# A state-space layer with pairwise scan products, reciprocal roots by power, one ring of nine buffers, and transfer prices and tie-breaks in its planner

## The chip, the cores and the metric

The kernel runs on one core of a Trainium2 chip. The metric is device time in microseconds (us) of one execution; lower is better. Five engines run side by side, each through its own instruction stream in order: TensorE (PE; its weight loads are shown as PEld), VectorE (DVE), ScalarE (ACT), GpSimd (POOL) and SyncE (SP), which here issues nearly all transfers.

## The reference, cut to what matters

Eight images of 384 channels and 1024 positions go through a state-space block and a small MLP, then through a second MLP with sign-binarised weights. All is float32.

```
t = layernorm(layernorm_c(x))                       # (8, 1024, 384)
xm, z = split(t @ in_proj_w.T)                      # 768 each
xc = silu(causal_conv3(xm) + conv_b)
dt, Bm, Cm = split(xc @ x_proj_w.T, [24, 40])
dt = softplus(dt @ dt_proj_w.T + dt_proj_b)
h_t = exp(dt_t * A) * h_{t-1} + (dt * xc)_t * Bm_t  # 768 channels x 16 states
y = (sum_n h * Cm + xc * D) * silu(z)
x = x + gelu(y @ out_proj_w.T @ mlp_w1.T + b1) @ mlp_w2.T + b2
t = t + bitlinear(gelu(bitlinear(layernorm(t))))    # W = sign(W - mean of its group)
```

`bitlinear` scales its result by the largest magnitude within an image and clips it. There are five such groups of one image each, so the last step is done for images 0 to 4 alone.

## The kernel before

The kernel first lists all work as operations (`Plan.add`: engine, price in us, what it reads and writes, which buffers it takes), and `Plan.run` then simulates the engines and writes the instructions out in the order that it finds. Nothing reorders them on the chip. An operation has a lane and an image number; `rank` orders the ready ones by lane, image and place in the list. PE's sums of scan results come first (lane -1), then the scans (lane 0), fronts of the next images, the MLPs, and the binarised MLP. Prices come from `c_act`, `c_dve`, `c_pool` and constants; a transfer holds a common line for size / 395e3 and lands 0.9 us later. A `Ring` is a set of equal buffers; a `Piece` is a tile that takes one when its first operation is issued. Where PE would stand for over 0.7 us, filler matmuls (tile `spare`, L412) are put in to hold its clock.

The stages, for each image b and halves of 512 positions:

- `s1`, the front. `norm` (L543 on) sums over channels on PE, and gets the reciprocal root by ACT's Sqrt (L587) and DVE's reciprocal (L590) on a 128x128 tile. Then come in_proj, the convolution, and Silu in place on one tile of six channel blocks (128x3072); x_proj (`p_dbc`); `p_bc` (L703), which lays out B and C rows; dt_proj, six matmuls of 128 rows (L722), of which only 2 x 24 rows matter, and Softplus. POOL multiplies xc by dt in place, 512 columns at a time (L732). xc, z, dt and dtx go to DRAM in one transfer each.
- `s2`, the scan. A unit is two tiles; a tile holds 32 channels x 4 states on 128 partitions and 1024 positions (images 0 and 7 run in halves, two channel groups of 512 to a tile). dt and dtx are read back with each row repeated for four states, B and C rows with each repeated for 32 channels. Per unit and quad of states, for each tile: ACT's exponential into PSUM (`da`, two buffers, L510), POOL's product u = dtx * B (L886), DVE's scan (L890), and the product with C: on POOL where `on_pool` says so (L904, scan written to u), otherwise on DVE (L907, scan written to da). PE sums four states with 32-column matmuls (`py`, L842).
- `s3`, out_proj and the first MLP; `ffn`, the binarised MLP, which stores y1 in DRAM, waits for its maximum, loads it again (`gf`), clips on POOL and applies Gelu; `binarise`, once, early.

Images 0 to 7 pass through these overlapped: under the scan of one image lie the front of later ones and the MLPs of earlier ones.

Of the kernel before, what the change touches and what calls it, by code (L numbers as in the profile page):

```python
# [33 lines left out]
P = 128  # L34
# [8 lines left out]
HK = KH // 2  # L43
T = 512
# [41 lines left out]

def c_act(n):
    return 0.25 + n * 0.00084


def c_dve(n):
    return 0.19 + n * 0.00102

# [36 lines left out]
class Piece:  # L130
# [8 lines left out]

    def __getitem__(self, part):  # L140
        return self, part

# [13 lines left out]
class Op:  # L156
    __slots__ = (
        "engine", "cost", "emit", "prio", "slack", "table", "size",
        "wants", "next", "ready", "tiles", "others", "settle",
# [3 lines left out]
class Plan:  # L163
# [12 lines left out]
    def add(self, engine, cost, emit, r=(), w=(), claim=(), table=None, size=0, others=None):  # L176
# [3 lines left out]
        op.size, op.prio = size, (*self.prio, len(self.ops))  # L180
# [40 lines left out]
    def run(self):  # L221
# [22 lines left out]
        def choose(e, now, able):  # L244
            able = [op for s, op in able if s <= now]
            if e == "ACT":
                same = [op for op in able if op.table == table and table != "exp"]
                plain = [op for op in able if op.table in (None, "exp")]
                able = same if table is not None and same else plain or able
            if e in ("DVE", "POOL"):  # L250

                able = [op for op in able if op.prio[0] > 0 and op.ready <= now - PATIENCE] or [
                    op for op in able if op.prio[0] == 0] or able
            return min(able, key=rank)

        def rank(op):
# [11 lines left out]
            return (*first, op.prio[2])  # L268
# [13 lines left out]
        while left:  # L282
# [49 lines left out]
            if e == "SP":  # L332
                dma_free = max(dma_free, end + 1.0) + op.size / 395e3
                end = dma_free + 0.9
# [17 lines left out]
class Layer:  # L352
    def __init__(self, ctx, tc, a, out):
# [9 lines left out]
        def ring(tag, bufs, where=sbuf):  # L363
# [7 lines left out]
            "front": ring("front", 2), "t_f": ring("t_f", 2), "w_f": ring("w_f", 3),  # L371
            "dbc": ring("dbc", 1), "halo": ring("halo", 2),

            "dt_r": ring("dt_r", 3), "dtx_r": ring("dtx_r", 3), "u": ring("u", 9),
# [4 lines left out]
            "yg": ring("yg", 1), "hid": ring("hid", 2), "t_b": ring("t_b", 1), "w_b": ring("w_b", 3),  # L379
            "w6": ring("w6", 2), "w6_n": ring("w6_n", 2), "res": ring("res", 2),  # L380

            "t_n": ring("t_n", 2), "small": ring("small", 7),

            "mm": ring("mm", 3, psum), "sq": ring("sq", 1),
            "rstd": ring("rstd", 2),
# [6 lines left out]
        for b in range(B):  # L392
            for name in ("dt", "dtx"):
                self.dram[name, b] = handed(f"{name}_d{b}", [DI, L])
# [24 lines left out]

    def constants(self):
        nc, a, const = self.nc, self.a, self.const
        small = const.tile([P, 3], F32, name="small")
        one, self.eps_m, self.eps_f = (small[:, i : i + 1] for i in range(3))
        for at, value in ((one, 1.0), (self.eps_m, E1 * E2), (self.eps_f, E_FFN)):
            nc.vector.memset(at, value)
# [8 lines left out]
        self.pick = const.tile([P, 2 * NS], F32, name="pick")  # L436
        nc.vector.tensor_add(self.pick, ident[:, DQ : 2 * DQ], ident[:, DP + DQ : DP + 2 * DQ])
        self.edge = const.tile([P, KD, 2], F32, name="edge")
# [23 lines left out]
    def load(self, to, view, src, r=(), size=0, cost=0.4):  # L462
# [3 lines left out]
            size=size,  # L466
        )

    def store(self, dst, frm, view, w, size, cost=0.4):
# [6 lines left out]
    def rows_moved(self, t, parts, move, r, w):  # L476
        n = P // len(parts)
        for i, mem in enumerate(parts):
            self.plan.add(
                "SP", 0.35, lambda i=i, mem=mem: move(t.real[i * n : (i + 1) * n, :], mem),  # L480
# [3 lines left out]
    def weights(self, ring, k, src, r=()):  # L484
        w = self.piece(ring, [P, k, P], ring)
        self.load(w, lambda t: t, src, r=r, size=4 * P * k * P, cost=0.34)
        return w

    def matmuls(self, p, w, t, k0, n, start, stop, r, claim, w0=0):


        def emit():
            for k in range(n):
                self.nc.tensor.matmul(  # L494
                    p.real, w.real[:, w0 + k, :], t.real[:, k0 + k, :],
# [47 lines left out]
    def norm(self, t, eps, scale):  # L543
# [17 lines left out]
        def spread(src, name):  # L561
            p = self.piece("mm", [P, T], name)

            def emit():
                for g in range(G):
                    one = self.ident[:, g * DQ : g * DQ + 1].to_broadcast([P, P])
                    nc.tensor.matmul(
                        p.real[:, g * TG : (g + 1) * TG], one, src.real, start=True, stop=True
# [16 lines left out]
        rstd = self.piece("rstd", [P, TG], "rstd")  # L585
        self.act(
            lambda: rstd.real, lambda: p_var.real, AF.Sqrt, c_act(TG), r=[p_var], w=[rstd],  # L587
            table="sqrt", bias=eps, scale=scale,
        )
        add("DVE", 0.93, lambda: nc.vector.reciprocal(rstd.real, rstd.real), w=[rstd])  # L590
        p_r = spread(rstd, "p_r")
# [6 lines left out]
    def s1(self, b):  # L598
# [3 lines left out]
        r_t, r_w, r_z, r_x = ("t_n", "w_b", "yg", "hid") if b == 1 else (  # L602
            "t_f", "w_f", "front", "front")

        def by_pair(name, half, t):
            d = self.dram[name, b]
            self.store(d.real[:, half].rearrange("k p l -> p k l"), t, lambda x: x, [d[half]],
                       4 * P * KD * T)

        def tiled(name, half, t):  # L610
            d = self.dram[name, b]
            to = d.real[:, HALVES[half]].rearrange("(k p) l -> p k l", p=P)
            self.store(to, t, lambda x: x, [d[half]], 4 * P * KD * T)

        def normed(half):
            t = self.piece(r_t, [P, KC, T], "t")
            src = a["x"][b][:, HALVES[half]].rearrange("(k p) l -> p k l", p=P)
            with self.plan.lane(14 if b == 1 else 4):
                self.load(t, lambda x: x, src, size=4 * P * KC * T)
                self.norm(t, self.eps_m, (1.0 + E2) / C)  # L620
# [7 lines left out]
        def gate(half, t):  # L628
            z = self.piece(r_z, [P, KD, T], "z")
            for m in range(KD):  # L630
                w = self.weights(r_w, KC, a["in_proj_w"][KD + m])
                pm = self.mm3(w, t, [t[k] for k in range(KC)], [z], "p_z")
                self.affine(
                    lambda m=m, z=z: z.real[:, m, :], lambda pm=pm: pm.real, [pm], [z[m]]
                )
            all_z = [z[m] for m in range(KD)]
            self.act(lambda z=z: z.real, lambda z=z: z.real, AF.Silu, c_act(KD * T),
                     r=[], w=all_z, table="silu")
            by_pair("z", half, z[0])

        for half, cols in enumerate(HALVES):
# [3 lines left out]
            xc = self.piece(r_x, [P, KD, T], "xc")  # L645
            for m in range(KD):
                w = self.weights(r_w, KC, a["in_proj_w"][m])
                pm = self.mm3(w, t, [t[k] for k in range(KC)], [xc], "p_in")
                tap = [self.conv_w[:, m, j : j + 1] for j in range(3)]
                self.affine(  # L650
                    lambda m=m, xc=xc: xc.real[:, m, :], lambda pm=pm: pm.real, [pm], [xc[m]],
# [7 lines left out]
                for s in (1, 2):  # L659
                    add("DVE", c_dve(T) + 0.06, lambda m=m, xc=xc, pm=pm, s=s, tap=tap: (  # L660
                        nc.vector.scalar_tensor_tensor(  # L661
                            xc.real[:, m, s:], pm.real[:, : T - s], tap[2 - s],
                            xc.real[:, m, s:], ALU.mult, ALU.add,
                        )
                    ), r=[pm], w=[xc[m]])
            if half:
                def edge(xc=xc):
                    tmp = self.edge
                    for s in (1, 2):
                        tp = tmp[:, :, :s]  # L670
                        w = self.conv_w[:, :, 2 - s : 3 - s].to_broadcast([P, KD, s])
                        nc.gpsimd.tensor_mul(tp, halo.real[:, :, 2 - s :], w)
                        nc.gpsimd.tensor_add(xc.real[:, :, :s], xc.real[:, :, :s], tp)

                add("POOL", 1.5, edge, r=[halo[m] for m in range(KD)],
                    w=[xc[m] for m in range(KD)])
            all_m = [xc[m] for m in range(KD)]
            self.act(lambda xc=xc: xc.real, lambda xc=xc: xc.real, AF.Silu, c_act(KD * T),
                     r=[], w=all_m, table="silu")
            by_pair("xc", half, xc[0])  # L680


# [4 lines left out]
            def low(w=w, xc=xc, p_dbc=p_dbc):  # L687
                for k in range(KC):
                    for i in range(2):
                        nc.tensor.matmul(  # L690
                            p_dbc.real[i * DP : (i + 1) * DP, :],
                            w.real[:, k, i * DP : (i + 1) * DP], xc.real[:, i * KC + k, :],
# [5 lines left out]
            p_bc = self.piece("mm", [P, TG], "p_bc")  # L698
            rows = self.piece("rstd", [P, TG], "rows")

            def both_halves(dbc=dbc, p_bc=p_bc):
                for g in range(G):
                    nc.tensor.matmul(  # L703
                        p_bc.real[g * DQ : (g + 1) * DQ, :], self.pick,
                        dbc.real[:, g * TG : (g + 1) * TG], start=True, stop=True,
                    )

            add("PE", 0.45, both_halves, r=[dbc], w=[p_bc], claim=[rows])
            self.affine(
                lambda rows=rows: rows.real, lambda p_bc=p_bc: p_bc.real, [p_bc], [rows], n=TG  # L710
            )
            d = self.dram["rows", b]
            for g in range(G):
                at = slice(cols.start + g * TG, cols.start + (g + 1) * TG)
                self.store(d.real[:, at], rows, lambda x, g=g: x[g * DQ : (g + 1) * DQ, :],
                           [d[half, g]], 4 * DQ * TG)
            dt = self.piece(r_x, [P, KD, T], "dt")
            for k in range(KD):
                if k % KC == 0:
                    w = self.weights(r_w, KC, a["dt_proj_w"][k // KC])  # L720
                pd = self.piece("mm", [P, T], "p_dt")
                add("PE", MM, lambda k=k, pd=pd, dbc=dbc, w=w: nc.tensor.matmul(  # L722
                    pd.real, w.real[:, k % KC, :], dbc.real, start=True, stop=True,
                ), r=[dbc, w], w=[pd], claim=[dt])
                self.affine(
                    lambda k=k, dt=dt: dt.real[:, k, :], lambda pd=pd: pd.real, [pd], [dt[k]],
                    self.dt_b[:, k : k + 1],
                )
            self.act(lambda dt=dt: dt.real, lambda dt=dt: dt.real, AF.Softplus, c_act(KD * T),
                     r=[], w=[dt[k] for k in range(KD)], table="softplus")  # L730
            for k in range(KD):
                add("POOL", c_pool(T), lambda k=k, xc=xc, dt=dt: nc.gpsimd.tensor_mul(  # L732
# [539 lines left out]
```

## Time and profile before

| | us |
|---|---|
| median of 3 runs | 3261.21 (3260.56 to 3263.69) |
| the profiled execution's own time | 3262.23 |
| its span, first to last instruction | 3260.4 |
| mean granted clock of PE | 0.984 |
| HBM traffic | 566 MB read, 180 MB written, 229 GB/s |
| ACT: 222 table loads | 284.8 |
| DVE: scans of 1024 / of 512 | 1310.2 / 470.4 |
| PE: products of p_h, p_o, p_out, p_in, p_z and both p_y | 2454.2 |
| PE: py, and fillers | 376.6, 80.0 |

Busy time is a sum over the instructions of a row; the engines work at the same time, so rows of different engines don't add. The lines of the profile themselves are shown with the steps that use them.

### The profile page before, as it was taken

How to read it: one execution, taken by the hardware profiler on the slowest of the kernel's cores; microseconds unless marked ns; L12 is line 12 of the kernel's file. 1: busy time of each engine (PE TensorE's matmuls, PEld its weight loads, DVE VectorE, ACT ScalarE, POOL GpSimd, SP SyncE). 2: the span in 40 equal slices, each digit the busy share in tenths (PEclk: the TensorE clock that was granted, in tenths of full speed). 3: DMA queues.
4: the chain of work that ended last, by engine and by line, in shares of the span. 5: the costliest groups of instructions: out<-in, count | busy, mean ns of one | idle time of the engine just before them, and what ended most of it. 6: DMA issues, size and time to landing. Idle time of an engine off the chain costs nothing.

```text
span 3260.4 us, 34027 instructions
## 1 busy us (share of the span) xinstructions
PE 3122.5 (96%) x11098; PEld 1317.7 (40%) x11098; DVE 2742.3 (84%) x2127; ACT 2024.3 (62%) x2246; POOL 2848.7 (87%) x1371
## 2 busy tenths in 40 slices
PE   8988999999999999999899999999999999999999
PEld 4333433444433434334334344343443534433334
DVE  4778899799978899888998878999788988789880
ACT  4778787656665576665656566755666565656551
POOL 1688899979999989999989999989999899999970
PEclk9998999999999999999999999999999999999999
DMA  6988778657796568675686667866677656766542
GB/s 218 305 282 276 249 250 294 221 183 234 259 322 197 184 230 291 229 238 197 208 298 211 237 211 246 295 225 226 220 275 250 207 185 205 249 187 207 167 141 76
DMA packets 367345, 748.73 MB, mean 230 GB/s; under 512 B 33856, under 2 KB 111168, under 8 KB 367168
## 3 DMA queue, kind: packets, MB, share of 16 engines
q1 hardware_dynamic: 366736, 746.46, 68.5%
q8 instruction: 89, 1.46, 0.2%
q14 instruction: 88, 0.72, 0.1%
q10 hardware_dynamic: 432, 0.09, 0.0%
HBM read 566.06 MB, written 180.36 MB: 229 GB/s over the span
## 4 chain that ended last, share of the span: by engine, by line
PE 74%; DMA 9%; DVE 6%; ACT 5%; issue 2%; POOL 2%; SPq 1%; ACTq 0%; DVEq 0%; POOLq 0%
PE p_y L494 17%; PE p_o L494 14%; PE p_h L494 13%; PE py L842 9%; PE p_out L494 6%; PE p_z L494 6%; PE p_in L494 5%; DVE da L890 2%; DMA w<-in_out_proj_w 2%; DMA w_f<-in_in_proj_w 2%; DVE u L890 1%; ACT L510 1%; DMA w_b<-in_mlp_w 1%; ACT da L510 1%; PE spare L412 1%
## 5 line engine op out<-in xcount | busy, mean ns | idle before, releaser
L886 POOL TENSOR_TENSOR u<-dtx_r,bc 128x1024 f32<-128x1024 f32 x768 | 1790.4, 2362 | 72.3 <-DMA dtx_r<-dtx_d 46.3
L510 ACT ACTIVATE da<-dt_r,a_neg 128x1024 f32<-128x1024 f32 (+1 forms) x960 | 902.7, 945 | 534.0 <-DVE u L907 331.1
L904 POOL TENSOR_TENSOR u<-u,bc 128x1024 f32<-128x1024 f32 x352 | 828.4, 2364 | 121.5 <-DVE u L890 115.5
L890 DVE TENSOR_TENSOR_SCAN da<-da,u 128x1024 f32<-128x1024 f32 (+1 forms) x416 | 840.5, 2020 | 111.6 <-POOL u L886 62.9
L890 DVE TENSOR_TENSOR_SCAN u<-da,u 128x1024 f32<-128x1024 f32 (+1 forms) x352 | 699.5, 2010 | 90.3 <-ACT da L510 63.0
L494 PE MATMUL p_h<-t,w_b 128*128 128x512 f32 x1152 | 513.6, 600 | 10.9 <-DMA w_b<-in_mlp_w 9.9
L907 DVE TENSOR_TENSOR u<-da,bc 128x1024 f32<-128x1024 f32 x416 | 507.9, 1221 | 10.5 <-ACT state L901 0.3
L494 PE MATMUL p_o<-g,w 128*128 128x512 f32 x1152 | 506.7, 595 | 5.4 <-ACT g L510 2.9
L842 PE MATMUL py<-u,fold 128*32 128x512 f32 x3072 | 376.6, 605 | 4.5 <-DVE u L907 4.5
L494 PEld LDWEIGHTS p_h<-t,w_b 128*128 128x128 f32 x1152 | 214.7, 190 | 298.1 <-issue 256.4
L494 PEld LDWEIGHTS p_o<-g,w 128*128 128x128 f32 x1152 | 215.9, 190 | 292.0 <-issue 277.3
L494 PE MATMUL p_y<-tn,w_b 128*128 128x512 f32 x720 | 324.9, 598 | 4.0 <-DVE tn L592 3.3
L494 PE MATMUL p_y<-gf,w_n 128*128 128x512 f32 x720 | 319.0, 599 | 6.7 <-DMA w_n<-bin_w 4.0
L510 ACT ACT_TABLE_LOAD x222 | 284.8, 1283 | 11.7 <-DVE xc L661 7.3
L494 PE MATMUL p_out<-yg,w 128*128 128x512 f32 x552 | 249.2, 604 | 8.9 <-DMA w<-in_out_proj_w 4.3
L494 PE MATMUL p_z<-t,w_f 128*128 128x512 f32 x504 | 232.5, 611 | 8.2 <-DMA w_f<-in_in_proj_w 6.2
L494 PE MATMUL p_in<-t,w_f 128*128 128x512 f32 x504 | 228.3, 602 | 10.8 <-DMA w_f<-in_in_proj_w 8.6
L494 PEld LDWEIGHTS p_y<-gf,w_n 128*128 128x128 f32 x720 | 135.1, 191 | 187.6 <-issue 172.4
L494 PEld LDWEIGHTS p_y<-tn,w_b 128*128 128x128 f32 x720 | 133.9, 190 | 183.9 <-issue 155.4
L842 PEld LDWEIGHTS py<-u,fold 128*32 128x32 f32 x3072 | 81.5, 110 | 261.1 <-issue 203.2
L525 ACT ACTIVATE g<-p_h,v_vecs 128x512 f32<-128x512 f32 x157 | 106.3, 681 | 120.9 <-PE p_h L494 120.7
L525 ACT ACTIVATE y<-p_y,v_vecs 128x512 f32<-128x512 f32 x138 | 94.1, 683 | 130.0 <-PE p_y L494 100.3
(112 smaller groups left out, 2700.3 us busy)
## 6 DMA issues: line engine op xcount, KB each, us to landing
dtx_r<-dtx_d SPq DMA_DIRECT2D x144, 512.0 KB, 5.8
dt_r<-dt_d SPq DMA_DIRECT2D x144, 512.0 KB, 6.0
w_b<-in_mlp_w SPq DMA_DIRECT2D x192, 192.0 KB, 2.9
w<-in_mlp_w SPq DMA_DIRECT2D x96, 384.0 KB, 3.6
w_f<-in_in_proj_w SPq DMA_DIRECT2D x168, 192.0 KB, 4.2
y_d<-y SPq DMA_DIRECT2D x120, 256.0 KB, 3.4
gf<-y_d SPq DMA_DIRECT2D x20, 1536.0 KB, 9.5
xc_d<-xc SPq DMA_DIRECT2D x16, 1536.0 KB, 7.3
```

Of the source, the lines that this page charges most:

```text
L412: self.plan.fill = lambda: self.nc.tensor.matmul(self.plan.spare.real[:, : 2 * P], self.ones, self.one.to_broadcast([P, 2 * P]), start=Tru ...
L494: self.nc.tensor.matmul(p.real, w.real[:, w0 + k, :], t.real[:, k0 + k, :], start=start and k == 0, stop=stop and k == n - 1,)
L510: lambda: self.nc.scalar.activation(out(), in_(), func, **{k: v() if callable(v) else v for k, v in kw.items()}),
L525: nc.scalar.activation(out(), in_(), AF.Identity, bias=bias, scale=scale)
L842: nc.tensor.matmul(py.real[p0 : p0 + DQ, :], self.fold, hc, start=False, stop=(q == NQUAD - 1), skip_group_check=True,)
L886: add("POOL", 2.36, lambda: nc.gpsimd.tensor_mul(u.real, dtx_r.real, spread(bq)), r=[dtx_r, bq], w=[u])
L890: add("DVE", (0.2 if half else 0.15) + n * 0.00209, lambda k=k, col=col: nc.vector.tensor_tensor_scan(to.real[:, k, :], da.real[:, k, :], ...
L904: add("POOL", 2.36, lambda: nc.gpsimd.tensor_mul(u.real, u.real, spread(cq)), r=[cq], w=[u])
L907: add("DVE", 1.21, lambda: nc.vector.tensor_mul(u.real, da.real, spread(cq)), r=[da, cq], w=[u])
```

## The change

Tiles of a unit become *pairs*: the two tiles' values lie interleaved, `[P, wide, n, 2]`, so that one POOL instruction multiplies both by one row of B or C, each element of which is used twice. dtx is stored interleaved too (`[KC, P, 2 * L]`) and read back in one transfer; a unit's channels are now every fourth one of 256. The scan reads and writes every other element. The fourth quad's u is written over dtx. `on_pool` gives POOL quads 0 and 2, and quad 1 in every fourth unit.

In `norm` the variance is scaled, turned by a small matmul to 128x4, an epsilon added, and raised to -0.5 on POOL; its spread uses the 128x4 columns as weights. dt_proj uses 32 rows per matmul, two at a time on different rows. The tiles of six blocks become three pieces of two (`Split`), with activations in place, stores and loads by piece; hid, yg and image 1's z share one ring of nine such pieces. `p_bc` and its four stores become one matmul (`p_all`) and one store. The column sums in `binarise` are taken three or four at a time. `gf` waits for its own y1 only. The planner gets transfer prices by kind (`land`), and `TURNS`: a number for each stretch of 100 us of planned time shifts an operation's place in the list by up to 16.

```diff
+STRETCH, REACH = 100, 16
+TURNS = (
+    19522, 59978, 49910, 0, 34827, 0, 6565, 14275, 0, 7565, 33371, 19911,
...
+def turned(n, by):
+    x = ((n + 1) * 2654435761 + by * 40503 * 65537) & 0xFFFFFFFF
+    x = ((x ^ x >> 15) * 2246822519) & 0xFFFFFFFF
+    return (x ^ x >> 13) % (2 * REACH + 1) - REACH
...
+def c_pair(n):
+    return 0.19 + n * 0.00188
...
-            return (*first, op.prio[2])
+            return (*first, op.prio[2] + (turned(op.prio[2], turn) if turn else 0))
...
-                dma_free = max(dma_free, end + 1.0) + op.size / 395e3
-                end = dma_free + 0.9
+                dma_free = max(dma_free, end + 0.5) + 0.05 + op.size / 360e3
+                end = dma_free + op.land
...
-            "front": ring("front", 2), "t_f": ring("t_f", 2), "w_f": ring("w_f", 3),
+            "front": ring("front", 7), "t_f": ring("t_f", 2), "w_f": ring("w_f", 3),
...
-            "dt_r": ring("dt_r", 3), "dtx_r": ring("dtx_r", 3), "u": ring("u", 9),
+            "dt_r": ring("dt_r", 3), "dtx_r": ring("dtx_r", 2), "u": ring("u", 3),
...
-            "yg": ring("yg", 1), "hid": ring("hid", 2), "t_b": ring("t_b", 1), "w_b": ring("w_b", 3),
-            "w6": ring("w6", 2), "w6_n": ring("w6_n", 2), "res": ring("res", 2),
+            "hid": ring("hid", 9), "t_b": ring("t_b", 1), "w_b": ring("w_b", 3),
+            "w6": ring("w6", 2), "w6_n": ring("w6_n", 2), "res": ring("res", 4),
...
+        rstd = self.piece("root", [P, G], "rstd")
+        add("DVE", 0.1, lambda: nc.vector.tensor_scalar_add(rstd.real, p_turned.real, eps),
+            r=[p_turned], w=[rstd])
+        add("POOL", 0.8, lambda: nc.gpsimd.tensor_tensor(
+            rstd.real, rstd.real, self.power.to_broadcast([P, G]), ALU.pow
+        ), w=[rstd])
...
+        def in_place(t, func, table):
+            parts = [t[k] for k in range(KD)]
+            for p, piece in enumerate(t.pieces):
+                mine = parts[p * PER : (p + 1) * PER]
+                self.act(lambda piece=piece: piece.real, lambda piece=piece: piece.real, func,
+                         c_act(PER * T), r=parts if p == 0 else mine, w=mine, table=table)
...
+                def two(k=k, pds=pds, dbc=dbc, ws=ws):
+                    for i in range(2):
+                        rows = slice(i * DQ, (i + 1) * DQ)
+                        nc.tensor.matmul(
+                            pds[i].real, ws[i].real[rows, (k + i) % KC, :], dbc.real[rows, :],
+                            start=True, stop=True,
+                        )
...
+                dtx = self.piece("sq", [P, T, 2], "dtx")
+                add("POOL", 2.35, lambda p=p, dtx=dtx, xc=xc, dt=dt: nc.gpsimd.tensor_mul(
+                    dtx.real.rearrange("p n i -> p i n"), xc.pieces[p].real, dt.pieces[p].real
...
-        return q == 0 or (q == 2 and (i == 0 or m % 3))
+        return q % 2 == 0 or (q == 1 and m % 4 == 0)
...
+        def product(t, x, row):
+            nc.gpsimd.tensor_mul(
+                u.real[:, x], t.real[:, x], row.real.unsqueeze(2).to_broadcast([P, n, 2])
+            )
```

## The prediction

> **What bounds the kernel now.** I read the engine totals first, then the chain of waits, then the busy time by stage, and last single groups and stretches of the timeline. Times are microseconds (us).
>
> ```profile
> PE 3122.5 (96%) x11098; PEld 1317.7 (40%) x11098; DVE 2742.3 (84%) x2127; ACT 2024.3 (62%) x2246; POOL 2848.7 (87%) x1371
> PE 74%; DMA 9%; DVE 6%; ACT 5%; issue 2%; POOL 2%; SPq 1%; ACTq 0%; DVEq 0%; POOLq 0%
> ```
>
> TensorE (PE) is nearly always busy and makes up three quarters of the chain that ends last. The stages (PE, PEld, DVE, ACT, POOL busy, then clock, DMA share, GB/s):
>
> ```profile
> 0.00:105.00 105.00, 90.77 (x444) 46.50 (x446) 43.04 (x61) 51.89 (x63) 12.67 (x18) 0.97 0.74 245
> 105.00:400.00 295.00, 265.03 (x1000) 111.27 (x998) 252.52 (x246) 229.11 (x309) 255.35 (x161) 0.95 0.83 272
> 400.00:1200.00 800.00, 769.47 (x2868) 322.36 (x2865) 714.99 (x536) 526.53 (x568) 734.95 (x339) 0.99 0.71 237
> 1200.00:2000.00 800.00, 768.54 (x2657) 317.76 (x2656) 701.50 (x498) 491.75 (x489) 753.41 (x343) 0.98 0.71 239
> 2000.00:2800.00 800.00, 779.63 (x2803) 337.36 (x2802) 698.09 (x493) 485.27 (x490) 742.29 (x339) 0.99 0.68 231
> 2800.00:3180.00 380.00, 372.61 (x1157) 148.71 (x1156) 329.17 (x294) 223.59 (x313) 350.09 (x175) 1.00 0.60 186
> 3180.00:3260.00 80.00, 76.50 (x180) 33.76 (x178) 3.00 (x4) 16.12 (x17) 0.00 (x0) 1.00 0.24 73
> ...
> 1200.00:1300.00 100.00, 94.21 (x356) 40.34 (x355) 96.68 (x76) 68.08 (x74) 95.77 (x45) 0.95 0.83 284
> ...
> 2000.00:2100.00 100.00, 91.36 (x420) 39.90 (x419) 95.96 (x69) 68.65 (x70) 88.23 (x46) 0.95 0.78 270
> 2100.00:2200.00 100.00, 98.62 (x343) 39.87 (x342) 94.89 (x76) 57.16 (x71) 89.61 (x39) 1.00 0.67 230
> ```
>
> Three parts follow. The head, 0 to 105, is the front of image 0 before the first scan product. The tail from 3180 is the last half image's MLP, which waits for the last scan. Between lie 3075 us in which the scans run on POOL, DVE and ACT under the matmuls. There PE is busy 265.0+769.5+768.5+779.6+372.6 = 2955 us, but the filler matmuls (tile spare, 80.0 us in all, 71.2 of it here) are gaps in disguise: real work is 2884, 93.8% of the stretch, and 191 us are gaps. POOL is busy 2836 (92.2%), DVE 2696 (87.7%). So PE sets the pace, with POOL close behind. PE's dips (91 and 94 us of 100) fall where DVE stands at 96 to 97 and the fronts load (270 to 284 GB/s).
>
> **The change, part by part.** The rows I price from:
>
> ```profile
> L886 POOL TENSOR_TENSOR u<-dtx_r,bc 128x1024 f32<-128x1024 f32 x768 | 1790.4, 2362 | 72.3 <-DMA dtx_r<-dtx_d 46.3 <-PE py L842 21.6 <-issue 2.4
> L904 POOL TENSOR_TENSOR u<-u,bc 128x1024 f32<-128x1024 f32 x352 | 828.4, 2364 | 121.5 <-DVE u L890 115.5 <-PE p_in L494 1.0 <-POOL u L886 0.6
> L1088 POOL TENSOR_SCALAR gf<-gf,q 128x3072 f32<-128x3072 f32 x20 | 57.9, 2898 | 11.2 <-DMA gf<-y_d 10.5 <-DVE u L890 0.7
> ...
> L907 DVE TENSOR_TENSOR u<-da,bc 128x1024 f32<-128x1024 f32 x416 | 507.9, 1221 | 10.5 <-ACT state L901 0.3
> L590 DVE RECIPROCAL rstd<-rstd 128x128 f32<-128x128 f32 x26 | 24.2, 937 | 1.8 <-ACT rstd L510 1.3
> ```
>
> Two stretches of PE's timeline and the last long piece of the chain (start, duration, group):
>
> ```profile
> 290.68 1.92 PE L842 MATMUL py<-u,fold 128*32 128x512 f32 x16
> 293.64 0.43 PE L703 MATMUL p_bc<-dbc,pick 128*32 128x128 f32 x8 [1.03 <-ACT dbc L523]
> ...
> 3194.70 30.90 PE p_h L494 x72
> ```
>
> The last of them gives the price of a full 128x512 product: 30.90/36 = 0.858 us (each is two instructions). The py line is eight 32-column products, four side by side: 1.92 against 2 x 0.858 = 1.72, so a group of narrow products costs 0.2 over its streaming time.
>
> *Pairs on POOL.* Before: 768 first and 352 second products, 2618.8 us. After: two channel groups interleaved in one tile. A full image has 48 pairs of first products and 24 + 3 of second ones (quads 0 and 2, and quad 1 of every fourth unit), 75 instructions of 2048 elements; six images make 450. Images 0 and 7 run in halves, 24 + 14 pairs a half, two instructions of 1024 a pair: 304 instructions. No row shows a product whose second operand repeats each element twice. From above by the plain rows: 1024 elements 2362, 512 elements 1275 (L732), so 2.123 ns an element and 0.188 fixed; 2048 take 4.54, and the sum is 450 x 4.54 + 304 x 2.362 = 2759, 140 more than before, because more second products go to POOL. From below by the one-operand row L1088, 0.943 ns an element: 2048 take 2.1. Between them stands the price that the planner is given in the diff, 0.19 + 0.00188 n, 4.04. Its other prices stand within 1% of their rows (1.21 for L907's 1.221, 0.93 for L590's 0.937, 2.36 for L886's 2.362), and a repeated operand should lie below the plain rate and above the one-operand rate, nearest the plain one. I take 4.04 (2.12 for 1024): 450 x 4.04 + 304 x 2.12 = 2461, so -158, with both ends kept for the range. The Trainium skill, page "GPSIMD Engine Reference", section "Elementwise — side-by-side cycle accounting", speaks against this: it puts a two-input product at about 2.6 cycles of 1.2 GHz an element whatever the operands, as both inputs share one read port; the 2.123 ns above are 2.55 cycles, so the trace agrees for plain operands, and by it a pair would cost about 4.6. What that makes of the time is the slow rival below.
>
> *Other POOL work.* The powers: 26 of 128x4; between a tiny POOL instruction (0.21, edge row) and a scan product (2.4); I take the planner's 0.8, +21. The dt product as 48 of 1024 instead of 96 of 512: 48 x 2.36 against 118.6, -5. Edges 48 instead of 32 at 0.21: +3. POOL in the stretch: 2836 - 158 + 19 = 2697.
>
> *DVE.* Products after the scan: 21 pairs a full image and 10 a half, two products each, give 6 x 42 + 4 x 20 = 332 instead of 416, 84 x 1.221 = -103. The 26 reciprocals (24 us) become 128x4 additions at some 0.15: -20. Scans are as many as before; they now step over every other element of u. If that cost 10% of a scan it would be +150 and DVE the bound; nothing in the rows suggests it, so I take 0. DVE in the stretch: 2573.
>
> *ACT.* A hundred in-place activations of 3072 (2.77) become 300 of 1024, about 1.05 by the 1536 row (1.48) and the 512 copies: +37. Gone are 26 roots (9) with 26 to 52 table loads of 1.28 (33 to 67). Near nothing, on an engine 62% busy; the cover is its 38% idle.
>
> *PE.* dt: 96 products (82.4) become 48 groups of two on different rows; if they run side by side, 48 x 1.06 = 50.9, -31 (bounds 0, if they queue, and -41). No row shows row groups side by side; the py line shows column groups so. p_bc 0.43 becomes one full product: 16 x 0.43 = +7. Sums of the binarised weights three or four at a time: 9 x 0.858 + 12 x 0.644 to 3 x 1.06 + 3 x 0.84, -10. The turn of the variance: 26 tiny products with a weight load (0.19) and drain, about 0.3, +8 (2 to 15). Together -26: real work 2858.
>
> *Norm chain.* Out go root, its load and reciprocal (2.6 us), in come a scale, a product, an addition and the power, which in POOL's order can sit behind one pair (4.0); behind it queue the next scan products, for which DVE waits. PE waited 10.5 us for rstd in 6 of 26 norms; 6 x 4 more would be +24 at worst. I take 0 over the gaps below, since the rest are made well ahead.
>
> *Rings, transfers, order.* The product of dt is no longer made in place but in the single buffer sq, so one must be stored (5.8, a 512 KB landing) before the next is made; this lies in fronts made ahead, except for image 0. There the scan now starts after one product and one 512 KB store instead of six products (7.7) and 1.5 MB (7.3): 7.7 - 2.4 + 7.3 - 5.8 = 7 us earlier, head 98. u holds 3 pairs and the last one lies in dtx: 4 pairs where 9 tiles held 4.5; POOL waited 21.6 us for PE to free u, and doubling that is +22 on an engine with 8% idle. SP issues 2092 transfers now and 164 more then (+128 for stores by pair, +120 for the halves' rows, +68 loads of yg and gf, +16 weights, -168 for rows, dt, dtx), at 0.33 to 0.53 each some +70 on a queue that mostly stands waiting for buffers; bytes grow 3 MB of 749. Hidden behind the weights' lead; without it DMA's 9% of the chain (290) grows by the same 8%, +23. The planner's new transfer prices and turned ties add no instruction. They can close or open gaps, at most those 191 us; I give them 0 by themselves.
>
> **Sum.** What remains is how the gaps answer. DVE loses 123 us (4.6%) and POOL 139 (4.9%), the two that are full where PE dips. In the undisturbed 100 us (2100) PE has 1.4 idle, so gaps are not PE's own. I take a third off: 191 to 125. Stretch 2858 + 125 = 2983; head 98, tail 80.4: span 3161. The profiled execution took 3262.2 for a span of 3260.4, 1.8 around it, and stands 1 us above the median of the runs. Forecast 3163. POOL would then be 90% busy in the stretch, DVE 86%, which leaves room.
>
> **Rivals.** *Gaps stay in proportion* (only PE's own work counts): 2858/0.938 = 3047, + 180 = 3227. For it: PE's gaps are scattered over dozens of small waits for weights, activations and norms, which the change does not shorten. Against: the dips where DVE is full.
>
> *Gaps almost close*, as in the best stretches (98.5% PE): 2858/0.985 = 2901, total 3083. For it: fillers between 2000 and 2800 alone are 46 us and show PE waiting for scans; against: the weights' transfers stay as they are.
>
> *POOL becomes the bound (slower).* The pair costs the plain rate, 4.54. POOL's stretch is 2836 + 140 + 22 = 2998. It has never been over 98.8% in 100 us and hardly over 95% over 800; at 96% the stretch is 3123 and the time 3305 (3270 at 97.2%, 3340 at 95%). It decides from the point where POOL's 2697 grow to 0.96 x 3075 = 2952, by 255 over 602 pairs, 0.42: a pair of 4.46. For it: the measured plain rate; against: the planner's price. By the Trainium skill's page cited above (about 4.6) this rival would hold.
>
> *The pairs on PE do not overlap and the ring of three pairs starves POOL:* +31 and +22 on the forecast, 3216, inside the range.
>
> **Chances.** Forecast 0.66 (own range 3105 to 3220), gaps in proportion 0.13, gaps close 0.08, POOL bound 0.11, and 0.02 for no change. A measurement of this kernel tells about 0.2% (6.5 us) from none. Faster 0.66 + 0.13 + 0.08 = 0.87, from which I give 0.01 to no change: 0.86, 0.03, 0.11. The range 3095 to 3250 leaves out the POOL rival and half of the one where gaps close.
>
> **What would show it.** Right: POOL products of 128x2048 near 4.04 and POOL below 2760 busy; 332 DVE products at 1.22 and scans still at 2.28; p_dt pairs of four instructions at 1.06; no reciprocal of 128x128; fillers and idle of PE together near 150 (218 now). Wrong: pairs over 4.46, POOL at 96% from 105 on and PE waiting on py; scans slower than 2.3; PE waiting for rstd over 30 us.

## The result, and the profile after

The changed kernel takes 3186.9 us (median of 4 runs, 3184.6 to 3200.4) against 3262.5 before: ratio 0.977, 95% interval 0.975 to 0.979. The forecast was 3163, range 3095 to 3250. So the sign and the range held, and 76 of the 99 us forecast came. The reason that I gave for most of them did not hold alone, as the experiments show.

Engine totals after, in the columns of the first fence of the prediction (the profiled execution took 3184.6, its span is 3182.5):

```profile
PE 3083.4 (97%) x10972; PEld 1274.9 (40%) x10972; DVE 2644.0 (83%) x2081; ACT 1966.5 (62%) x2363; POOL 2744.8 (86%) x1046
```

The groups that answer to the priced ones (line, engine, output and inputs, form, count; busy us and mean ns; idle before and what ended it):

```profile
L942 POOL TENSOR_TENSOR u<-dtx_r,bc 128x2048 f32<-128x2048 f32 x216 | 880.6, 4088 | 107.2 <-PE py L907 66.7 <-issue 22.5 <-DMA bc<-rows_d 8.1
L942 POOL TENSOR_TENSOR u<-u,bc 128x2048 f32<-128x2048 f32 x162 | 661.5, 4087 | 45.3 <-DVE u L967 45.3
...
L644 POOL TENSOR_TENSOR rstd<-rstd,small 128x4 f32<-128x4 f32 x26 | 26.4, 1016 | 31.1 <-DVE rstd L642 28.9 <-DVE mean L1146 1.4 <-DMA y_d<-y 0.9
...
L967 DVE TENSOR_TENSOR_SCAN u<-da,u 128x1024 f32<-128x1024 f32 x324 | 738.9, 2284 | 94.5 <-POOL u L942 48.7 <-ACT da L556 35.0 <-ACT z L556 0.8
L987 DVE TENSOR_TENSOR dtx_r<-da,bc 128x1024 f32<-128x1024 f32 x144 | 174.6, 1222 | 2.9
...
L451 PE MATMUL spare<-small 128*128 128x256 f32 x228 | 58.1, 394 | 0.0
L783 PE MATMUL p_dt<-dbc,w_f 32*128 32x512 f32 x168 | 55.1, 690 | 5.3 <-ACT dbc L569 2.7 <-DVE tn L628 1.1 <-DVE t L648 1.0
```

A pair costs 4.088, the scan still 2.284, the power 1.016, and POOL now waits for PE to free u (66.7 in this row alone, 21.6 in the corresponding row before). The stages in which the scans run in full (columns as in the prediction):

```profile
400.00:1200.00 800.00, 779.07 (x2879) 319.78 (x2877) 692.54 (x522) 514.38 (x600) 703.23 (x236) 0.98 0.73 246
1200.00:2000.00 800.00, 789.60 (x2814) 325.84 (x2812) 697.52 (x505) 480.79 (x525) 735.35 (x227) 1.00 0.73 245
2000.00:2800.00 800.00, 794.30 (x2708) 328.21 (x2707) 695.49 (x504) 497.69 (x554) 750.58 (x245) 1.00 0.73 245
```

PE stands at 97 to 99% there, 96 to 97% before. I split PE's time into real work (busy less fillers) and gaps (idle plus fillers). Before: 3122.5 - 80.0 = 3042.5 work, 3260.4 - 3042.5 = 218 gaps. After: 3025.3 and 157. So of 78 us of span, 17 are work and 61 are gaps; the question is what closed the gaps.

### The profile page after: what moved, and what is told of

Same layout as the page of the kernel before. It is cut to its first block, busy times and chain, and to the rows that moved or that the text cites. A ratio compares the mean times of both kernels' runs of the same rounds, so it can differ in the third digit from the quotient of the medians.

```text
span 3182.5 us, 33759 instructions
## 1 busy us (share of the span) xinstructions
PE 3083.4 (97%) x10972; PEld 1274.9 (40%) x10972; DVE 2644.0 (83%) x2081; ACT 1966.5 (62%) x2363; POOL 2744.8 (86%) x1046
## 5 line engine op out<-in xcount | busy, mean ns | idle before, releaser
L942 POOL TENSOR_TENSOR u<-dtx_r,bc 128x2048 f32<-128x2048 f32 (+1 forms) x360 | 1185.5, 3308 | 124.9 <-PE py L907 79.7
L942 POOL TENSOR_TENSOR u<-u,bc 128x2048 f32<-128x2048 f32 (+1 forms) x274 | 900.1, 3290 | 86.9 <-DVE u L967 81.4
L967 DVE TENSOR_TENSOR_SCAN u<-da,u 128x1024 f32<-128x1024 f32 (+1 forms) x436 | 869.1, 2007 | 127.1 <-POOL u L942 71.4
L967 DVE TENSOR_TENSOR_SCAN da<-da,dtx_r 128x1024 f32<-128x1024 f32 (+1 forms) x192 | 386.3, 2019 | 55.6 <-POOL dtx_r L942 34.2
L942 POOL TENSOR_TENSOR dtx_r<-dtx_r,bc 128x2048 f32<-128x2048 f32 (+1 forms) x120 | 396.8, 3311 | 2.4
L907 PE MATMUL py<-u,fold 128*32 128x512 f32 x2304 | 303.5, 628 | 0.2 <-POOL u L942 0.2
L967 DVE TENSOR_TENSOR_SCAN da<-da,u 128x1024 f32<-128x1024 f32 (+1 forms) x140 | 283.7, 2041 | 13.7 <-POOL u L942 6.9
```

What stands on the lines that cost most here:

```text
L907: nc.tensor.matmul(py.real[g * DQ : (g + 1) * DQ, :], self.fold, hc, start=False, stop=(q == NQUAD - 1), skip_group_check=True,)
L942: nc.gpsimd.tensor_mul(u.real[:, x], t.real[:, x], row.real.unsqueeze(2).to_broadcast([P, n, 2]))
L967: da=da, in_u=in_u: nc.vector.tensor_tensor_scan(to(i), da.real[:, i, :], in_u(i), state.real[:, col : col + 1] if half else 0.0, ALU.mult ...
```

## The experiments

Each kernel is the changed one with the edit shown, unless it says otherwise. A *table* is the list `TURNS`. "Fitted" means that numbers were tried for one stretch after another and those kept that made the planner's own plan shortest. Ratios are to the kernel before, run beside it, with 95% intervals; the changed kernel is at 0.977. Times of different experiments are from different occasions, so ratios compare better than medians.

**The table emptied, and other numbers.**

```diff
-TURNS = (19522, 59978, 49910, 0, 34827, ...)
+TURNS = ()                                      # no_turns
+TURNS = (19523, 59979, 49911, 0, 34828, ...)    # other_turns
```

> The changed kernel with its table of numbers emptied, so that ties go by place in the list as before; all else as changed. My theory (the loads taken off POOL and DVE by the pairs let PE's gaps shrink; the order of ties adds little): 3187 grows to at most 3210. Rival (the table carries most of the gain, and the pairs alone are worth little): over 3230, that is at least 45 of the 75 us gained go.

> The same table with 1 added to every number that is not zero, so other shifts of the same size. My theory: any order does about as well, 3175 to 3215. Rival (it is these numbers that matter): over 3230, no better than without a table.

Measured: 3251.9, ratio 0.995 (0.993 to 0.997), and 3288.0, 1.008 (1.005 to 1.010). Both rivals held; my theory fell. Without the table, with all pairs, rings, powers and transfer prices in place, 1.8 of the 2.3 points are gone (65 us between the medians), and with other numbers it is slower than before. The totals and fillers of the kernel without a table:

```profile
PE 3136.1 (96%) x11128; PEld 1310.5 (40%) x11128; DVE 2641.4 (81%) x2076; ACT 1981.2 (61%) x2369; POOL 2750.0 (85%) x1051
...
L447 PE MATMUL spare<-small 128*128 128x256 f32 x384 | 100.2, 398 | 2.1 <-DVE z L572 1.2 <-ACT z L565 0.9
```

POOL is relieved as after (2750) and DVE too, yet the gaps are 3252.0 - (3136.1 - 100.2) = 216: in all, not closed. What POOL waited for, the table-less kernel first, the kernel before last (us in all, times, longest):

```profile
POOL u L938 <- PE py L903: 100.6, 45, 10.6
POOL u L938 <- DVE u L963: 88.0, 52, 7.2
```

```profile
POOL u L904 <- DVE u L890: 115.5, 70, 10.6
...
POOL u L886 <- PE py L842: 21.6, 11, 5.3
```

POOL's busy time fell by 99 us, and its waits for PE to free a buffer of u rose by 79. In the changed kernel they are 79.7 too, with far smaller gaps, so they alone don't keep PE's gaps open.

The sum of 216 hides where gaps closed and opened. Busy time and fillers from 400 to 2800, first without a table, then in the changed kernel:

```profile
sum 2400.00, PE 2352.25 PEld 983.36 DVE 2047.13 ACT 1468.78 POOL 2146.67; mean PE 784.08 PEld 327.79 DVE 682.38 ACT 489.59 POOL 715.56
sum 2400.00, PE 72.18; mean PE 24.06
```

```profile
sum 2400.00, PE 2362.97 PEld 973.84 DVE 2085.55 ACT 1492.86 POOL 2189.16; mean PE 787.66 PEld 324.61 DVE 695.18 ACT 497.62 POOL 729.72
sum 2400.00, PE 31.43; mean PE 10.48
```

The gaps there are 2400 - 2352.25 + 72.18 = 120 and 2400 - 2362.97 + 31.43 = 69, against 144 before. So the change without its table closed 24 us in the middle, and 22 opened at the ends. The same working for all stretches, with kernels of the next experiments (us of gaps):

| kernel | 0 to 105 | 105 to 400 | 400 to 2800 | from 2800 | all |
|---|---|---|---|---|---|
| before | 22 | 39 | 144 | 13 | 218 |
| before, with a fitted table | 25 | 52 | 122 | 16 | 215 |
| changed, no table | 20 | 55 | 120 | 21 | 216 |
| changed, other numbers | 19 | 56 | 122 | 45 | 242 |
| changed, my table | 21 | 43 | 93 | 23 | 180 |
| changed, given table | 21 | 51 | 69 | 17 | 157 |
| plain products, fitted table | 18 | 47 | 115 | 76 | 255 |

**A second theory**: relief and order need each other. The order can close gaps only where POOL has room, and the room is used only by a fitted order. The rival is that a fitted table does it on any kernel.

**A table of its own for the kernel before, and for the changed one.** The first is the kernel before with only this added; the second the changed kernel with a table fitted afresh.

```diff
-            return min(able, key=rank)
...
+            at = int(now / STRETCH)
+            turn = TURNS[at] if at < len(TURNS) else 0
+            return min(able, key=lambda op: rank(op, turn))
...
-            return (*first, op.prio[2])
+            return (*first, op.prio[2] + (turned(op.prio[2], turn) if turn else 0))
```

> The kernel before with the change's turning of ties added and a table of its own, fitted to its plan; nothing else of the change. Theory A, formed after the first runs (the two need each other: the table can close gaps only where POOL and DVE have idle time, which the pairs make): 10 to 30 us off the kernel before, ratio 0.990 to 0.997. Theory B (the table alone does it, on any kernel, as its 65 of 75 us suggest): 55 or more off, ratio at most 0.983.

> The changed kernel with another table, fitted to its plan afresh from an empty one. Theory A (a fitted order is worth some 50 us on this structure, whichever numbers give it): 3195 to 3215, ratio 0.978 to 0.986. Theory C (the given numbers were picked by the chip's time or are luck, a fit to the plan is worth little on the chip): 3235 or more, ratio over 0.990.

Measured: 3249.7, 0.9945 (0.993 to 0.996), and 3214.7, 0.9835 (0.982 to 0.985). Both came as the second theory expected, and its rival fell. A fitted table is worth 0.55% on the old structure and 1.2 (my table) to 1.8 points (the given one) on the new, where the structure alone is worth 0.5%. Alone the two make 0.55 + 0.49 = 1.0%, together 1.65 to 2.3%. That they need each other is shown less firmly than that both are needed for the whole gain: with my table the excess over the sum is 0.6 points, no more than fitted tables differ by below, and from 400 to 2800 relief (24 us) and table (22) by themselves make 46 of the 51 that closed with both. My other tables, in the kernels with pairs below, closed 49 to 73 there, the given one 75. The totals and fillers of the kernel before with a table, then of the changed kernel with mine:

```profile
PE 3122.6 (96%) x11134; PEld 1321.4 (41%) x11134; DVE 2740.1 (84%) x2127; ACT 2016.5 (62%) x2240; POOL 2852.9 (88%) x1375
...
L429 PE MATMUL spare<-small 128*128 128x256 f32 x350 | 91.4, 403 | 0.0
```

```profile
PE 3099.3 (96%) x10984; PEld 1282.7 (40%) x10984; DVE 2647.2 (82%) x2083; ACT 1964.0 (61%) x2358; POOL 2749.7 (86%) x1051
...
L451 PE MATMUL spare<-small 128*128 128x256 f32 x240 | 64.5, 409 | 0.0
```

Gaps are 3246.0 - 3122.6 + 91.4 = 215 in the first, hardly fewer than the 218 without (22 closed in the middle, 13 opened from 105 to 400), and 3214.3 - 3099.3 + 64.5 = 180 in the second.

A rival is left: the changed kernel's planner also has new transfer prices, and the planner before has not, so a plan fitted there may simply tell less of the chip. The kernel with plain products below speaks against it: it has the new prices and a fitted table, but no relief, and its gaps in the middle are 115, near the 122 of the old kernel with a table.

**The pair taken away, twice.** First in the same order with the same prices, then with POOL's old share of second products, the planner's price of two plain products, and a fitted table.

```diff
-            nc.gpsimd.tensor_mul(
-                u.real[:, x], t.real[:, x], row.real.unsqueeze(2).to_broadcast([P, n, 2])
-            )
+            for i in range(2):
+                nc.gpsimd.tensor_mul(u.real[:, x, :, i], t.real[:, x, :, i], row.real)
```

> Each pair product as two instructions, one per tile, the row of B or C read plainly; same order of everything, same prices in the planner. Theory: each costs the plain 2.36 for 1024 and 1.28 for 512, so POOL gains 378 x ... = some 600 pair products x 0.65 = 390 us, from 2745 to about 3135 busy; POOL becomes the bound and the time is 3135/0.95 + 110 = 3400 (3300 to 3450). Rival (PE stays the bound and POOL's idle time takes it): under 3250.

> The changed kernel with each pair product as two plain ones, POOL's share of second products as before (352 tiles), and a table fitted to its plan. Theory A (the cheap pair is what makes room): POOL gets 1120 x 2.42 instead of 2482 us, some 190 more, DVE 98 more, both about as full as before the change, and the coarser buffers are paid for nothing: 3300 to 3340, slower than before. Theory B (the table does it): under 3230.

Measured: 3406.1, 1.043 (1.038 to 1.048), and 3312.2, 1.013 (1.011 to 1.015). As expected both times. In the first kernel POOL is the bound:

```profile
PE 3183.3 (94%) x10972; PEld 1296.9 (38%) x10972; DVE 2645.8 (78%) x2081; ACT 1967.4 (58%) x2363; POOL 3180.5 (93%) x1800
...
L943 POOL TENSOR_TENSOR u<-dtx_r,bc 128x1024 f32<-128x1024 f32 x432 | 1031.3, 2419 | 39.3 <-PE py L907 28.8 <-issue 8.5 <-POOL dtx_r L943 1.2
```

Two plain products make 4.84, above the 4.46 from which the prediction let POOL decide. In the second kernel a fitted table does not make up for it:

```profile
PE 3178.7 (96%) x11240; PEld 1338.9 (40%) x11240; DVE 2757.2 (83%) x2180; ACT 1974.3 (60%) x2365; POOL 2979.9 (90%) x1681
```

Without the cheap pair the rest of the change is a loss. It is not the pair's price alone: both tiles still share buffers and waits, and POOL is 131 us fuller than before the change, 102 of it in products of the same tiles, which now step over every other element (2.419 for 2.362) and are split into 512 in images 0 and 7.

**POOL's old share with the pairs.**

```diff
-        return q % 2 == 0 or (q == 1 and m % 4 == 0)
+        return q == 0 or (q == 2 and m % 6 != 0)
```

> The changed kernel with POOL's share of second products as before (352 tiles instead of 436) and a table fitted to its plan: POOL 42 pairs or 172 us less, DVE 84 products or 103 us more, both against the changed kernel. If DVE is what holds PE's gaps open (they fell where DVE was full before): 3235 or more. If POOL is: under 3200. If the two are in balance: like the changed kernel with its own fitted table, 3205 to 3225.

Measured: 3210.5, 0.984 (0.981 to 0.987), as expected if the two are in balance.

```profile
PE 3109.4 (97%) x11064; PEld 1296.0 (40%) x11064; DVE 2739.6 (85%) x2150; ACT 1977.8 (62%) x2390; POOL 2576.4 (80%) x984
```

DVE is as full as in the kernel before (2742), and yet this kernel is 1.1 points faster than that one with a fitted table (3249.7, POOL 2852.9). So the relief of DVE, on which I had built half of the forecast, isn't needed where POOL is relieved by more, while the kernels with plain products show what a fuller POOL costs. A difference below the spread of fitted tables, some 20 us, would not show here.

**The powers back on ACT and DVE**, with a fitted table, and then with that table refined.

```diff
...
-        add("POOL", 0.8, lambda: nc.gpsimd.tensor_tensor(
-            rstd.real, rstd.real, self.power.to_broadcast([P, G]), ALU.pow
-        ), w=[rstd])
...
+            lambda: rstd.real, lambda: p_var.real, AF.Sqrt, c_act(TG), r=[p_var], w=[rstd],
+            table="sqrt", bias=self.eps[eps], scale=scale,
+        )
+        add("DVE", 0.93, lambda: nc.vector.reciprocal(rstd.real, rstd.real), w=[rstd])
...
```

> The changed kernel with the reciprocal root by ACT's Sqrt and DVE's reciprocal again, and a table fitted to its plan. By my prediction's step (the power on POOL worth nothing over the gaps, -20 us on DVE, +8 on PE): within 10 us of the changed kernel with its own fitted table. Rival (the powers free ACT of table loads and the chain of norms of waits, and that carries part of the gain): 20 us or more slower than that.

> Sqrt and reciprocal as in roots_own_table, its table refined further, as the best candidate for a version that beats both kernels. If the powers on POOL carry none of the gain and a table is worth what it closes on the plan: 3178 to 3190, ratio 0.973 to 0.977, level with the changed kernel or a little ahead. Rival (the given kernel's powers are worth something that the refinement doesn't reach): 3195 or more.

Measured: 3193.2, 0.977 (0.975 to 0.980), and 3183.9, 0.976 (0.974 to 0.979). Against the changed kernel with my table (0.9835) the first is some 20 us faster, not the same as expected: either tables fitted in the same way differ by that much, or the roots are better than the powers; one table each can't tell. Either way the powers aren't needed for the gain: with the roots the time is that of the changed kernel, with these table loads (first of the two kernels) where the changed kernel has 172:

```profile
L558 ACT ACT_TABLE_LOAD x209 | 268.1, 1283 | 3.7
```

ACT stands at 62 to 63% in all of them, so the loads cost nothing that shows. The refined kernel (0.976) is level with the changed one.

**Rows of dt_proj in one group**, same order.

```diff
-                        rows = slice(i * DQ, (i + 1) * DQ)
+                        rows = slice(0, DQ)
```

> The changed kernel in the same order, but both matmuls of each p_dt pair use rows 0 to 31, so that they can't run side by side. My prediction's step (31 us of PE work saved by the overlap, one for one on the path): p_dt back from 64 to some 90 us, and 3200 to 3220, ratio 0.981 to 0.987. Rival (the gain of single PE instructions is hidden in gaps): within 8 us of 3187.

Measured: 3210.0, 0.983 (0.980 to 0.986), with these rows:

```profile
L783 PE MATMUL p_dt<-dbc,w_f 32*128 32x512 f32 x168 | 89.9, 655 | 3.9 <-ACT dbc L569 2.3 <-DVE tn L628 0.6 <-DVE t L648 0.5
...
L783 PE MATMUL p_dt<-dbc,w_b 32*128 32x512 f32 x24 | 14.3, 713 | 2.6 <-ACT var L571 2.1 <-ACT mean L571 0.4
```

PE's work for dt grows from 64.1 (55.1 + 9.0 after) to 104.2, more than the 90 expected, and the time by 19 us (by the ratios) to 23 (by the medians). The time lies in the range of my step and not of its rival, but one for one does not hold: with the order held, PE's own work is on the path for about half, and the gaps take much of the rest (157 after, 3209.5 - (3126.0 - 59.0) = 142.5 here).

**The ring of nine split.**

```diff
-            "hid": ring("hid", 9),
...
+            "hid": ring("hid", 6), "yg": ring("yg", 3),
...
```

> The changed kernel with the ring of nine split into six for hid and three for yg and image 1's z, and a table fitted to its plan. My prediction gave the rings nothing: 3205 to 3225, like the changed kernel with its own fitted table. Rival (the shared ring lets the MLPs run over each other and closes gaps): 3235 or more.

Measured: 3218.8, 0.9855 (0.982 to 0.989). The same as with one ring and a table of mine (0.9835), within the spread of tables: the ring by itself is worth nothing that shows; a gain below some 20 us would not.

**Sums over contiguous values.**

```diff
-  parts = [u.real[:, 0, h, i] for i in both for h in HALVES] ...
+  parts = [u.real[:, 0].rearrange("p n i -> p (n i)")[:, k * T : (k + 1) * T] for k in range(4)] ...
```

> PE's sums read each tile u as it lies in memory instead of every other element, so the two tiles' values get mixed in the sums and y is not the layer's; count, size, order and waits of the instructions stay. Theory (reading every other element is what made a py matmul 609 ns at least where it was 592): back to 592 and 1.92 for sixteen, some 0.12 x 192 = 23 us less PE work, and 3160 to 3175 if PE's work is on the path. Rival (the new order of the column groups made it slower): 609 stays and the time too, 3180 to 3195.

Measured: 3177.7, 0.973 (0.970 to 0.977), 9 us below the changed kernel and in neither expected range, though the intervals overlap. A gain in time is likely but not shown: at a granted clock of 0.988 one execution here spans 3169.9 and two of the changed kernel 3182.5 and 3183.2, but the profiled one here ran at 0.984, spans 3184.2, and saves only 2 us of PE's work in all. The rows of the sums, here and in the changed kernel:

```profile
L907 PE MATMUL py<-u,fold 128*32 128x512 f32 x2304 | 291.5, 609 | 0.1
```

```profile
L907 PE MATMUL py<-u,fold 128*32 128x512 f32 x2304 | 303.5, 628 | 0.2 <-POOL u L942 0.2
```

The shortest instruction is 592 ns here as before the change, and 609 in the changed kernel: of the two expectations for the row, that of the stride holds: reading every other element is what costs there. The sums are 392.7 with the row for dtx (101.2), against 407.6.

**Not tried alone**: the transfer prices, the sums of binarised weights, more buffers for u.

## Why the prediction was right, and where it was not

**Prices: nearly all right.** Pair 4.04 us forecast, 4.088 measured; POOL's products 2461 forecast, 2482 measured (880.6 + 661.5 above, and 940.2 in the other four forms). DVE's 332 products at 1.22, scans unchanged, table loads 50 fewer, p_turned 9 for 8. dt is -29 for -31, but from 93.3 to 64.1, where I had 82.4 to 50.9: the row before was not at 0.858 a product, and a group of four instructions takes 1.34 on the mean (64.1/48), not 1.06. The Trainium skill, page "GPSIMD Engine Reference", section "Elementwise — side-by-side cycle accounting", has about 2.6 cycles an element for two inputs, by which, as an estimate, a pair would be 4.6 us. From 2.137 for 1024 to 4.088 for 2048 it is 1.91 ns an element here, 2.3 cycles of 1.2 GHz, so the measurement differs from the page where each element of one operand is used twice.

**Terms mis-sized.** The products (+21), the clip in pieces (not priced; 70.6 for 57.9) and the power (1.016 for 0.8) leave POOL at 2745 and not at some 2710. p_all cost +12 for +7. The sums on PE were taken at no change; they cost +31 (376.6 to 407.6), of which 15 are the stride. PE's work fell by 17 instead of 26. Of the lesser sums, 2048 elements at 0.943 ns make 1.93 and not 2.1, and POOL at 97.2% makes 3264 and not 3270; nothing hangs on either.

**The step that failed** is in the sum: "I take a third off: 191 to 125", because "DVE loses 123 us (4.6%) and POOL 139 (4.9%), the two that are full where PE dips"; and before it, of the planner's ties, "I give them 0 by themselves". The first rests on dips picked from the profile. Others as deep lie where DVE is far from full (columns as in the prediction):

```profile
200.00:300.00 100.00, 83.28 (x357) 36.30 (x357) 82.70 (x81) 80.06 (x120) 80.05 (x51) 0.90 0.87 284
...
1300.00:1400.00 100.00, 92.17 (x301) 37.33 (x300) 88.45 (x62) 59.92 (x52) 93.19 (x41) 0.97 0.67 234
```

Without the table, the rest of the change took 24 us off the gaps from 400 to 2800, a sixth of them and not a third, and gave 22 back outside (216 in all instead of 218). The rival *gaps in proportion*, 3227, describes that kernel best, and even it is 25 us too low. The table, put at 0, closed 59, 216 to 157. That the size came out near is luck: the third had no working behind it, and it was close to what the relief and a fitted order gained together, of which the forecast had only the relief as the cause. The pairs are still necessary: the same kind of table gained 18 us on the kernel before, and with plain products the time is 3312.

**The buffers of u.** I allowed POOL's wait for PE to double from 21.6. It went to 79.7 after and 100.6 without a table. Whether the coarser buffers are what keeps the relief from showing stays open: no run has more of them.

**The slow rival** was right in kind: with plain pairs POOL decides, 3406 measured at 4.84. Its price, 3305 at 4.54, is not tested, since no run has such a pair. It took POOL's share of its stretch as 96%. The share was 98.0% in the given order (3149.9 of the 3215 us from 105 to 3320) and 94.3% with POOL's old share and a fitted table (2946.7 of the 3125 from 105 to 3230).

**The wait for powers** stayed small, 3.9 us in three waits of PE, for the at most 24 more that I bounded it by. POOL itself stood 28.9 us waiting for the power's input, five times, which the prediction had not.

## What to carry to other kernels

Where a program's order is fixed beforehand, judge the relief of a full engine and the order of instructions together: here the pairs showed most of their worth only once the order was fitted to them, and taking a part out must be measured with a fitted order, or with the order held. Tie-breaks alone moved this kernel by 100 us (3187 to 3288), more than any part taken out alone but the pairs, so a comparison of two structures under one order each says little below a per cent. Split a sum of gaps by stretch before saying that nothing closed. When an engine is freed, look next at which buffer it now waits for.

## What the runs showed of the hardware that I had not expected

- GpSimd multiplies faster where one operand repeats each element: 4.088 us for 2048, against 2.36 for 1024 plain ones and 2.419 for 1024 with every other element read and written.
- A float32 matmul of 32 columns takes 609 ns at least when it reads every other element, 592 when contiguous. The scan on DVE does not mind (2.284 us and 2.285). The Trainium skill, page "SBUF — State Buffer", section "Specifications (TRN2)", asks for two hits in a 16-byte line for full bandwidth, which this stride meets; DVE agrees, PE and GpSimd here pay 2 to 3%.
- Two matmuls on different groups of 32 rows run side by side: four instructions take 1.34 us on the mean (1.13 in one stretch of PE's timeline), and 2.17 (104.2/48) when they share a group.
- A power of 128x4 values takes 1.016 on GpSimd, where a product of 128x6 takes 0.21.
